# Decoder layer with 160 routed experts: two lists of expert blocks, the first beside the last row; few-pair experts four to a block; weighted y rows scattered by pair

## The chip, the cores and the metric

The kernel runs on one core of a Trainium2 chip. The metric is device time of one execution in microseconds (us); lower is better. The kernel before takes 1595.51 us, the median of three runs (1593.03 to 1595.99).

## What is computed

Eight sequences ("rows", b = 0 to 7) of 256 tokens with 256 features go through a Mamba block, a cross attention with a feed-forward network, and a mixture of experts, each with a residual and a layer norm. All arithmetic is float32. The change touches the third part:

```
logits = x @ router_w.T + expert_bias[None, :]          # 2048 tokens, 160 experts
top_w, top_idx = jax.lax.top_k(sigmoid(logits), 8)
top_w = top_w / (sum(top_w) + 1e-09) * 2.5
...
h1 = silu(einsum('th,eih->eti', x, w_gate))              # 128 hidden units per expert
routed = einsum('eti,ehi->th', h1 * combine.T[:, :, None], w_down)
shared = silu(x @ w_gate_shared.T) @ w_down_shared.T
x = layernorm(x + routed + shared)
```

Each token picks 8 of 160 experts, so there are 16,384 (token, expert) pairs. How they fall on the experts is fixed by the inputs. Counted from the reference's routing:

| pairs of an expert | experts |
|---|---|
| none | 44 |
| at least one | 116 |
| sum over experts of whole blocks of 128 pairs | 97 blocks |
| remainder after whole blocks 1 to 32 | 72 |
| remainder 33 to 127 | 44 |
| whole blocks of 128 from the first six rows alone | 69 blocks |

Whole blocks and remainders together make 97 + 116 = 213 blocks. The trace of the kernel before agrees with this count: its gathers move packets of four token rows, and of the packets that are only partly filled 31 hold one row, 34 two and 23 three, the numbers that these remainders give.

## The kernel before

Three stages follow one another.

The front (up to 905 us) runs a scan over 8 rows times 16 states. While row b is scanned, the later parts of row b-1 (`rest`, a generator that yields some 35 times: output projection, attention, feed-forward, router) are put between the scan's steps by hand: `manual_schedule` fixes the order of PE (TensorE), ACT (ScalarE), DVE (VectorE) and POOL (GpSimd). `rest` ends with the routing of its row: `so_far` holds the number of pairs of each expert so far, `placei` the place of each pair in the table `tab_d` (2048 places per expert), and `scatter` writes the pair numbers there with 16 indirect DMAs a row (L619). After the last scan step the remainder of row 6's `rest` and the whole of row 7's `rest` run alone, then the last 32 scatters.

Then the list of blocks is made (L697 to L779): how many blocks of 128 pairs each expert has, which expert and which table row each block is, and the table rows themselves, fetched by three indirect DMAs `got` (L760).

The block stage runs `USUAL` = 216 blocks in eight lanes. `fetch(i)` reads the expert's number into SP's register, loads its 256 KB of weights `we` by SP (skipped where the lane's previous block had the same expert), and gathers the 128 token rows `xg` with an indirect DMA of POOL (L799). `block(i)` transposes them on PE (`bt`, copied to `bx` by DVE), multiplies by the gate weights (`bh`, `Silu` on ACT into `bg`), multiplies by the down weights (`by`), copies to `bo` by DVE or ACT and stores 128 rows of `y_d` by SP (L827). Blocks 217 and up stand in a `tc.If` that runs only where more than 216 are needed; here 213 are.

Last, for every 128 tokens, eight indirect DMAs on POOL (L903) bring back the eight y rows of each token, and PE sums them, weighted by diagonal matrices `diags` (L909), with the shared expert (L907); then a layer norm and the output.

Of the kernel before, what the change touches and what calls it, by code (L numbers as in the profile page):

```python
# [14 lines left out]
P = 128  # L15
# [19 lines left out]
NBLK = T * TOPK // P + NE  # L35
QB = -(-NBLK // P)
LANES = 8
USUAL = T * TOPK // P + NE // 2 + LANES
PER = T // P
BIG = float(1 << 20)  # L40
# [21 lines left out]
def decoder_layer(  # L62
# [24 lines left out]
    pools = {}  # L87
    small = ctx.enter_context(tc.tile_pool(name="small", bufs=4))
# [8 lines left out]
    y_d = dram.tile([NBLK * P, D], F32, name="y_d")  # L97
    tab_d = dram.tile([NE * T, 1], F32, name="tab_d")

    tab_views = dram_disjoint_views(tab_d, NTT * TOPK)  # L100


    wts_all = keep.tile([P, NTT, TOPK], F32, name="wts_all")
    which_all = keep.tile([P, NTT, TOPK], F32, name="which_all")
    place_all = keep.tile([P, NTT, TOPK], F32, name="place_all")
    first_place = keep.tile([P, NE], F32, name="first_place")
    nc.gpsimd.iota(first_place, pattern=[[T, NE]], base=0, channel_multiplier=0, allow_small_or_imprecise_dtypes=True)
# [7 lines left out]
    pair_no = keep.tile([P, NTT, TOPK], F32, name="pair_no")  # L115
    nc.gpsimd.iota(
        pair_no, pattern=[[P * TOPK, NTT], [1, TOPK]], base=0, channel_multiplier=TOPK,
# [11 lines left out]


    def exps():
        return nc.scalar.preload_act_table_set("natural_log_exp_and_others")

    def scaling(src, name):
# [8 lines left out]
        for c in range(TT):  # L143
            nc.vector.bn_aggr(mv[:, c, :], st[:, c, :])  # L144
        nc.scalar.activation(rs, mv[:, :, 1], AF.Ln, bias=eps)  # L145
# [26 lines left out]
    with ExitStack() as first:  # L172
        wts = first.enter_context(tc.tile_pool(name="wts", bufs=1))
        m1 = first.enter_context(tc.tile_pool(name="m1", bufs=1))
        m2 = first.enter_context(tc.tile_pool(name="m2", bufs=2))
        m3 = first.enter_context(tc.tile_pool(name="m3", bufs=3))
        m4 = first.enter_context(tc.tile_pool(name="m4", bufs=4))
        pools["ps"] = first.enter_context(tc.tile_pool(name="ps_front", bufs=2, space=PSUM))
        acc = first.enter_context(tc.tile_pool(name="acc_front", bufs=2, space=PSUM))
        held = first.enter_context(tc.tile_pool(name="held", bufs=1, space=PSUM))  # L180
        a1 = first.enter_context(tc.tile_pool(name="a1", bufs=1))
        a2 = first.enter_context(tc.tile_pool(name="a2", bufs=2))
        dr = first.enter_context(tc.tile_pool(name="dr", bufs=2, space=bass.MemoryType.DRAM))

# [27 lines left out]
        def fill():  # L212


            w = none.shape[-1]
            v = tab_d.rearrange("(i p n) o -> p i (n o)", p=P, n=w // 2)
            nc.sync.dma_start(v, none[:, None, : w // 2].to_broadcast([P, NE * T * 2 // (P * w), w // 2]))
            nc.sync.dma_start(
                y_d[USUAL * P :, :].rearrange("(p a n) d -> p a (n d)", p=P, n=w // D),
                none[:, None, :].to_broadcast([P, (NBLK - USUAL) * D // w, w]),  # L220
            )
# [3 lines left out]
        exps()  # L225
# [19 lines left out]
        def head(b, xt, made):  # L245
# [35 lines left out]
            for j in range(KI // 2):  # L281
                pz = projected(KI // 2 + j)
                yield
                nc.scalar.copy(sz[:, 2 * j : 2 * j + 2, :], pz)
            nc.scalar.activation(u, u, AF.Silu)
            nc.scalar.activation(sz, sz, AF.Silu)
            exps()
# [33 lines left out]
            nc.scalar.preload_act_table_set("natural_log")  # L321
            nc.scalar.activation(delta, delta, AF.Ln)  # L322
            exps()
# [57 lines left out]
        def rest(b, sz, ya):  # L381
# [77 lines left out]
            nc.scalar.activation(top, top, AF.Identity, scale=-scale)  # L459
            total = small.tile([P, TT], F32, tag="total", name=f"total_{b}")  # L460
# [79 lines left out]
            nc.sync.dma_start(x3_d[b * S : (b + 1) * S, :].rearrange("(c p) d -> p c d", p=P), x3)  # L540
            yield
# [15 lines left out]
            nc.vector.tensor_add(pr, pl, mid(rv[:, R_EB : R_EB + NE], TT))  # L557
            nc.scalar.activation(pr, pr, AF.Sigmoid)
            exps()
# [27 lines left out]
            place = place_all[:, b * TT : (b + 1) * TT, :]  # L587
            placei = small.tile([P, TT, TOPK], mybir.dt.int32, tag="placei", name=f"placei_{b}")
            expert = small.tile([P, TT, TOPK], mybir.dt.int32, tag="expert", name=f"expert_{b}")
            for c in range(TT):  # L590
                at = pn[:, c * NE : (c + 1) * NE]
                key = a1.tile([P, NE], F32, tag="key", name=f"key_{b}_{c}")
                nc.vector.scalar_tensor_tensor(key, at, 1.0, chosen[:, c, :], ALU.add, ALU.mult)
                nc.vector.max(place[:, c, :], key)
# [3 lines left out]
            ordered = which_all[:, b * TT : (b + 1) * TT, :]  # L598
            nc.vector.tensor_copy(ordered, expert)
            scattered.append(scatter(b, placei))  # L600
            yield
            for c in range(TT):
# [7 lines left out]
                nc.vector.tensor_reduce(wts_all[:, i, :], match, AX.X, ALU.add)  # L610
                nc.vector.tensor_scalar(
                    wts_all[:, i, :], wts_all[:, i, :], den[:, c : c + 1], ROUTED_SCALE, ALU.mult, ALU.mult
                )

        def scatter(b, placei):
            for c in range(TT):
                for j in range(TOPK):
# [3 lines left out]
                        in_=pair_no[:, i, j : j + 1], in_offset=None,  # L621
# [14 lines left out]
        E_ = mybir.EngineType  # L636
        with tc.manual_schedule(engines={E_.PE, E_.Activation, E_.DVE, E_.Pool}):
# [4 lines left out]
            ahead = 0  # L642
            for i, (b, n) in enumerate(steps):
# [32 lines left out]
            rests.append(rest(B - 1, made["sz"], made["ya"]))  # L676
            while rests:
                go(rests)
            while scattered:
                go(scattered)  # L680


    I32 = mybir.dt.int32
    blk = ctx.enter_context(tc.tile_pool(name="blk", bufs=1))
    pools["ps"] = ctx.enter_context(tc.tile_pool(name="ps", bufs=4, space=PSUM))
    acc = ctx.enter_context(tc.tile_pool(name="acc", bufs=4, space=PSUM))
    b2 = ctx.enter_context(tc.tile_pool(name="b2", bufs=2))
    b3 = ctx.enter_context(tc.tile_pool(name="b3", bufs=3))
    b4 = ctx.enter_context(tc.tile_pool(name="b4", bufs=4))

    sh = blk.tile([P, KD * P + D], F32, name="sh")
    nc.sync.dma_start(sh, shared)
    nblk = blk.tile([P, NE], F32, name="nblk")
    nblki = blk.tile([P, NE], I32, name="nblki")
    upto = blk.tile([P, NE], F32, name="upto")
    total = bank("total")[:, :NE]
    nc.tensor.matmul(total, ones, so_far, start=True, stop=True)  # L697
    nc.vector.tensor_sub(nblk, total, first_place)
    nc.vector.tensor_scalar_add(nblk, nblk, float(P - 1))
    nc.vector.tensor_copy(nblki, nblk)  # L700
    nc.vector.tensor_single_scalar(nblki, nblki, 7, op=ALU.logical_shift_right)
    nc.vector.tensor_copy(nblk, nblki)
    nc.vector.tensor_tensor_scan(upto, ones[:, 0:1].to_broadcast([P, NE]), nblk, 0.0, ALU.mult, ALU.add)


    moved = blk.tile([P, NE], F32, name="moved")
    nc.vector.tensor_sub(moved, upto, nblk)
    nc.vector.scalar_tensor_tensor(moved, moved, float(P), first_place, ALU.mult, ALU.subtract)
    slot = blk.tile([P, NTT, TOPK], F32, name="slot")
    sloti = blk.tile([P, NTT, TOPK], I32, name="sloti")  # L710


    turn = blk.tile([P, QB], I32, name="turn")
    nc.gpsimd.iota(turn, pattern=[[P, QB]], base=0, channel_multiplier=1)
    lanei = blk.tile([P, QB], I32, name="lanei")
    nc.vector.tensor_single_scalar(lanei, turn, LANES - 1, op=ALU.bitwise_and)
    nc.vector.tensor_single_scalar(turn, turn, LANES.bit_length() - 1, op=ALU.logical_shift_right)
    step = blk.tile([P, QB], F32, name="step")
    nc.vector.tensor_copy(step, turn)
    block_no = blk.tile([P, QB], F32, name="block_no")  # L720
    nc.vector.tensor_copy(block_no, lanei)
    leni = blk.tile([P, 1], I32, name="leni")
    lane_len = blk.tile([P, 1], F32, name="lane_len")
    nc.vector.tensor_scalar_add(lane_len, upto[:, NE - 1 : NE], float(LANES - 1))
    nc.vector.tensor_copy(leni, lane_len)
    nc.vector.tensor_single_scalar(leni, leni, LANES.bit_length() - 1, op=ALU.logical_shift_right)
    nc.vector.tensor_copy(lane_len, leni)
    lane_ends = blk.tile([P, LANES], F32, name="lane_ends")
    for i in range(LANES):
        nc.vector.tensor_scalar_mul(lane_ends[:, i : i + 1], lane_len, float(i + 1))  # L730
    nc.vector.scalar_tensor_tensor(
        block_no, block_no, lane_len, step, ALU.mult, ALU.add
    )
    past = blk.tile([P, QB], F32, name="past")
    nc.vector.tensor_scalar(past, step, lane_len, float(2 * NBLK), ALU.is_ge, ALU.mult)
    nc.vector.tensor_add(block_no, block_no, past)
# [46 lines left out]
    for t in xg:  # L783
        nc.gpsimd.memset(t, 0.0)
# [88 lines left out]
    for i in range(LANES - 1):  # L873
        fetch(i)
    for i in range(USUAL):
# [5 lines left out]
        if i == 8 * NTT:  # L881
            slots()
# [100 lines left out]
```

## Time and profile before

| what | us |
|---|---|
| median of three runs | 1595.51 |
| the profiled execution | 1594.16 |
| its span, first to last instruction | 1592.3 |
| PE busy in the span | 1147.9 (72%) |
| DVE busy | 895.6 (56%) |
| POOL busy | 881.4 (55%) |
| ACT busy | 664.0 (42%) |
| mean granted TensorE clock | 0.852 |

The shares are averages over stages that are bound by different things, so they say little by themselves. Times in the profile count from the start of the span. A group of instructions is listed as line, engine, operation, output<-input, shape and count, then total busy time and mean of one in ns, then the time its engine sat idle just before it and what ended that.

### The profile page before, as it was taken

Reading aid. Unit: us, or ns where it says so; the run is one execution under the profiler, and the core shown is the slowest. Engines: PE = TensorE matmul, PEld = TensorE weight load, DVE = VectorE, ACT = ScalarE, POOL = GpSimd, SP = SyncE. Lnnn points to the kernel's source line nnn. Section 1 sums busy time; section 2 is a strip of 40 time slices with the busy share of each in tenths; the row PEclk is TensorE's granted clock in tenths of the full one; section 3 lists DMA queues with packets and bytes.
Section 4 is the critical chain, followed back from the end, with each engine's and each line's share of the span. In section 5 each row is a group of like instructions: output and inputs, shape, how many; then the busy total and the mean of one; then the engine's idle time right before and its main releaser. Section 6 shows DMA issues by size and latency. Waiting matters only on the chain. (4 is left out here: it accounts for less than half of the span.)

```text
span 1592.3 us, 16270 instructions
## 1 busy us (share of the span) xinstructions
PE 1147.9 (72%) x4283; PEld 751.5 (47%) x4283; DVE 895.6 (56%) x1786; ACT 664.0 (42%) x1532; POOL 881.4 (55%) x713
## 2 busy tenths in 40 slices
PE   4367877787786787787777755038888888877776
PEld 2123544455354454454444444026666666653433
DVE  2478789678668677767868532649633333320000
ACT  4264664744755655654744423002222222212221
POOL 1545464574574655744847302656566666637775
PEclk8588989888798898888888977559999999987776
DMA  9611202112112211111120000036777778644443
GB/s 319 230 60 53 80 34 64 43 60 40 41 60 47 47 47 54 25 55 41 35 71 27 16 5 13 1 100 203 218 223 210 217 209 251 209 130 131 131 133 93
DMA packets 110292, 160.30 MB, mean 101 GB/s; under 512 B 20756, under 2 KB 77622, under 8 KB 110192
## 3 DMA queue, kind: packets, MB, share of 16 engines
q1 hardware_dynamic: 89488, 125.37, 25.5%
q0 software_dynamic: 20704, 33.81, 7.9%
q14 instruction: 63, 0.52, 0.2%
q8 instruction: 37, 0.61, 0.2%
HBM read 152.28 MB, written 43.58 MB: 123 GB/s over the span
## 5 line engine op out<-in xcount | busy, mean ns | idle before, releaser
L373 PE MATMUL ya<-h,ident 128*128 128x512 f32 x512 | 297.2, 711 | 135.2 <-DVE h L368 135.1
L343 POOL TENSOR_TENSOR g<-du,bc 128x1024 f32<-128x1024 f32 x128 | 300.0, 2355 | 95.1 <-DVE states L358 73.9
L358 DVE TENSOR_TENSOR_SCAN states<-decay,g 128x512 f32<-128x512 f32 x256 | 314.5, 1229 | 60.2 <-ACT decay L348 20.9
L348 ACT ACTIVATE decay<-delta,na 128x255 f32<-128x255 f32 x512 | 237.9, 474 | 136.1 <-DVE states L358 125.0
L799 POOL DMA_INDIRECT xg<-x_d,tokens x216 | 216.3, 1001 | 130.6 <-PE bt L810 120.3
L373 PEld LDWEIGHTS ya<-h,ident 128*128 128x128 f32 x512 | 107.6, 223 | 258.4 <-DVE h L368 141.3
L812 DVE COPY bx<-bt 128x256 f32<-128x256 f32 x216 | 92.0, 426 | 179.9 <-PE bt L810 179.1
L821 PE MATMUL by<-we,bg 128*128 128x256 f32 x432 | 151.1, 432 | 44.0 <-ACT bg L819 35.5
L819 ACT ACTIVATE bg<-bh 128x128 f32<-128x128 f32 x216 | 60.0, 278 | 247.3 <-PE bh L815 244.2
L368 DVE TENSOR_TENSOR h<-states,bc 128x1024 f32<-128x1024 f32 x128 | 156.1, 1219 | 4.9
L903 POOL DMA_INDIRECT y<-y_d,sloti x128 | 121.1, 946 | 57.9 <-issue 36.0
L619 POOL DMA_INDIRECT tab_d<-pair_no,placei x128 | 128.9, 1007 | 38.1 <-issue 29.7
L909 PE MATMUL yn<-y,diags 128*128 128x256 f32 x256 | 112.9, 554 | 39.6 <-DMA y<-y_d,sloti 38.4
L815 PEld LDWEIGHTS bh<-bx,we 128*128 128x128 f32 x864 | 129.8, 193 | 20.5 <-DVE bx L812 10.0
L815 PE MATMUL bh<-bx,we 128*128 128x128 f32 x864 | 134.6, 279 | 4.1 <-DVE bx L812 2.8
L821 PEld LDWEIGHTS by<-we,bg 128*128 128x128 f32 x432 | 65.2, 189 | 96.3 <-ACT bg L819 95.7
L909 PEld LDWEIGHTS yn<-y,diags 128*128 128x128 f32 x256 | 56.5, 259 | 93.6 <-DMA y<-y_d,sloti 89.4
L256 PE MATMUL pj<-xt,in_sb 128*128 128x256 f32 x256 | 74.8, 445 | 26.9 <-DVE u L275 14.8
L910 DVE TENSOR_TENSOR xs<-xs,yn 128x512 f32<-128x512 f32 x8 | 5.5, 688 | 157.6 <-PE yn L909 157.6
L810 PE MATMUL bt<-ident,xg 128*128 128x128 f32 x432 | 83.5, 275 | 3.8 <-DMA xg<-x_d,tokens 3.8
L256 PEld LDWEIGHTS pj<-xt,in_sb 128*128 128x128 f32 x256 | 56.5, 226 | 46.3 <-issue 15.8
L324 POOL TENSOR_TENSOR delta<-delta,e 128x1024 f32<-128x1024 f32 x8 | 18.8, 2347 | 97.7 <-ACT delta L322 97.7
(215 smaller groups left out, 1660.0 us busy)
## 6 DMA issues: line engine op xcount, KB each, us to landing
we<-in_experts_dram SPq DMA_DIRECT2D x216, 256.0 KB
bc<-bc_d SPq DMA_DIRECT2D x64, 512.0 KB
y_d<-bo SPq DMA_DIRECT2D x216, 128.0 KB
y_d<-none SPq DMA_DIRECT2D x1, 9216.0 KB
xg<-x_d,tokens POOLq DMA_INDIRECT x216, 3.8
xt<-in_x_t_dram SPq DMA_DIRECT2D x8, 256.0 KB
w_sb<-in_w_dram SPq DMA_DIRECT2D x2, 1024.0 KB
xn<-in_x_dram SPq DMA_DIRECT2D x8, 256.0 KB
```

The lines of the kernel that those rows point to most:

```text
L256: nc.tensor.matmul(pj[:, e, :], in_sb[:, k, o : o + P], xt[:, k, :], start=(k == 0), stop=(k == KD - 1))
L343: nc.gpsimd.tensor_mul(g, made["du"], mid(made["b_rows"][:, n % NG, :], KI))
L348: nc.scalar.activation(decay[k // 2][:, k % 2, 1:], made["delta"][:, k, 1:], AF.Exp, scale=na[:, k * NS + n : k * NS + n + 1],)
L358: nc.vector.tensor_tensor_scan(states_f[:, part], decay[j].rearrange("p k t -> p (k t)"), gf[:, part], 0.0, ALU.mult, ALU.add)
L368: nc.vector.tensor_mul(h, states, mid(made["c_rows"][:, n % NG, :], KI))
L373: nc.tensor.matmul(ya[j], ident, hf[:, j * NT : (j + 1) * NT], start=(n == 0), stop=(n == NS - 1))
L619: nc.gpsimd.indirect_dma_start(out=tab_views[i * TOPK + j], out_offset=bass.IndirectOffsetOnAxis(ap=placei[:, c, j : j + 1], axis=0), in_= ...
L799: nc.gpsimd.indirect_dma_start(out=xg[i % LANES], out_offset=None, in_=x3_d, in_offset=bass.IndirectOffsetOnAxis(ap=tokens[:, i : i + 1], ...
L815: nc.tensor.matmul(ph, w[:, k * P : (k + 1) * P], xt[:, k * P : (k + 1) * P], start=(k == 0), stop=(k == KD - 1))
L821: nc.tensor.matmul(py, g, w[:, KD * P :], start=True, stop=True)
L903: nc.gpsimd.indirect_dma_start(out=y8[:, j, :], out_offset=None, in_=y_d, in_offset=bass.IndirectOffsetOnAxis(ap=sloti[:, i, j : j + 1], a ...
L909: nc.tensor.matmul(pn[:, c, :], diags[:, i, j, :], y8[:, j, :], start=False, stop=(j == TOPK - 1))
```

## The change

Pairs now carry their weight: `pair_all` holds (pair number, weight) and `tab_d` is twice as wide; the weight arithmetic moves ahead of the scatter in `rest`. `y_d` has one row per pair (16,384 rows) in place of one per block slot.

Blocks come from two times and three kinds. List a: whole blocks of 128 pairs of the first six rows, at most `FIRST` = 68, made while row 7 is scanned. List b: the whole blocks that are left after all eight rows, and the remainders above `FEW` = 32 pairs, one block each; 64 of them (`USUAL`) always run. List c: remainders of 1 to 32 pairs, four experts to a block (`GROUP`); 20 such blocks (`USUAL_FEW`) always run. What b and c hold beyond that is run by a `tc.If`, which goes through all the slots that are left of both lists, whatever their number.

After the scan and the remainder of row 6's `rest`, the three first steps of row 7's `rest` run, the scan's memory is given up, and the blocks start. Row 7's `rest`, the scatters of rows 6 and 7 and the making of lists b and c are links of a chain, about one of which is put after each block of list a. One turn `s` issues, in order, the fetch for a later turn, the transposes of turn s+2, the gate product of s+1, the down product of s and the store of s-1. Every block loads its own weights, into 12 buffers; 8 buffers hold gathered rows. The y rows are scaled by the weight when they leave PSUM and are scattered to the row of their pair by an indirect DMA of POOL (the SP store is gone). The shared expert's part is added to `base` beside list b. At the end one plain DMA of 2 MB a row brings the y rows in pair order, and DVE sums the eight of each token.

The core of the diff, with the new functions:

```diff
+AFTER = B - 2
+FIRST = 68
+FEW = 32
+GROUP = P // FEW
+MOST = T * TOPK // P + NE
+USUAL = 64
+USUAL_FEW = 20
...
+    y_d = dram.tile([T * TOPK, D], F32, name="y_d")
+    tab_d = dram.tile([NE * T, 2], F32, name="tab_d")
...
+        def first_list():
...
+            nc.vector.tensor_copy(wholei, counted("a", some))
+            nc.vector.tensor_single_scalar(wholei, wholei, P.bit_length() - 1, op=ALU.logical_shift_right)
...
+            nc.vector.scalar_tensor_tensor(done, done, 0.0, whole, ALU.max, ALU.min)
+            lists["done"] = done
+            yield
+            yield from listed("a", 0, ends, whole, None, P, some, blk)
+        def other_lists(kept, temps):
...
+            nc.vector.scalar_tensor_tensor(cnt, done, float(-P), cnt, ALU.mult, ALU.add)
...
+            nc.vector.scalar_tensor_tensor(nblk, left, float(FEW), whole, ALU.is_gt, ALU.add)
+            upto(ends, nblk)
...
+            nc.vector.tensor_scalar_add(rest_of, ends[:, NE - 1 : NE], float(-USUAL))
+            nc.vector.tensor_scalar_add(few_rest, few_ends[:, NE - 1 : NE], float(-USUAL_FEW * GROUP))
+            nc.vector.tensor_tensor(rest_of, rest_of, few_rest, ALU.max)
+            nc.vector.tensor_scalar(rest_of, rest_of, 0.0, 1.0, ALU.max, ALU.add)
+            resti = kept.tile([P, 1], I32, name="resti")
+            nc.vector.tensor_copy(resti, rest_of)
+            lists["more"] = resti
...
+            def fetch(turn):
...
+                for g in range(needs(turn)):
+                    w = we[used[0] % NW]
...
+                    nc.sync.dma_start(
+                        w, experts[bass.ds(ev, 1), :, :].rearrange("o p n -> p (o n)"),
+                        bounds_check="skip_entire_dma",
+                    )
...
+                nc.gpsimd.indirect_dma_start(
+                    out=xi, out_offset=None, in_=src,
+                    in_offset=bass.IndirectOffsetOnAxis(ap=tokens[:, i : i + 1], axis=0),
...
+            def inner(turn):
...
+                for g, w in enumerate(t["ws"]):
+                    for k in range(KD):
+                        nc.tensor.matmul(
+                            ph[:, g * n : (g + 1) * n], w[:, k * P : (k + 1) * P],
+                            t["xt"][:, k * P + g * n : k * P + (g + 1) * n], start=(k == 0), stop=(k == KD - 1),
+                        )
...
+            def outer(turn, odd):
...
+                for g, w in enumerate(t["ws"]):
+                    nc.tensor.matmul(
+                        py[g * n : (g + 1) * n, :], t["g"][:, g * n : (g + 1) * n], w[:, KD * P :], start=True, stop=True
+                    )
...
+                if odd:
+                    nc.scalar.activation(t["y"], py, AF.Identity, scale=t["wt"])
+                else:
+                    nc.vector.tensor_scalar_mul(t["y"], py, t["wt"])
+            def store(turn):
...
+                nc.gpsimd.indirect_dma_start(
+                    out=y_views[view], out_offset=bass.IndirectOffsetOnAxis(ap=t["pairs"], axis=0),
+                    in_=t["y"], in_offset=None, bounds_check=T * TOPK - 1, oob_is_err=False,
+                )
+            def go_through(turns, between):
+                n = len(turns)
+                fetched = 0
+                for s in range(-2, n + 1):
+                    while fetched < min(n, max(s, 0) + NX - 1) and (
+                        sum(needs(t) for t in turns[max(s, 0) : fetched + 1]) <= NW
+                    ):
+                        fetch(turns[fetched])
+                        fetched += 1
+                    if 0 <= s + 2 < n:
+                        turn_x(turns[s + 2])
+                    if 0 <= s + 1 < n:
+                        inner(turns[s + 1])
+                    if 0 <= s < n:
+                        outer(turns[s], s % 2)
+                    if 0 <= s - 1 < n:
+                        store(turns[s - 1])
+                    between(s)
+            usual = [("a", i) for i in range(FIRST)] + [("b", i) for i in range(USUAL)]
+            usual += [("c", i) for i in range(USUAL_FEW)]
+            chain = [rests, scattered, [other_lists(kept, temps)]]
...
+            go_through(usual, beside)
...
+    more = nc.values_load(lists["more"][0:1, 0:1], min_val=1, max_val=MOST + NE)
+    with tc.If(more > 1):
+        with tc.manual_schedule(engines={E_.PE, E_.Activation, E_.DVE, E_.Pool}):
+            for kind in ("b", "c"):
+                for q in range(1, -(-MOST // P) if kind == "b" else -(-NE // P)):
+                    for _ in listed(kind, q, *lists[kind]):
+                        pass
+            turns = [("b", i) for i in range(USUAL, MOST)] + [("c", i) for i in range(USUAL_FEW, NE // GROUP)]
+            go_through(turns, lambda s: None)
...
+            nc.sync.dma_start(
+                y8, y_d[b * S * TOPK : (b + 1) * S * TOPK, :].rearrange("(c p j) d -> p c j d", p=P, j=TOPK)
             )
+            on = y8s.tile([P, TT, D], F32, tag="on", name=f"on_{b}")
+            nc.vector.tensor_reduce(on, y8.rearrange("p c j d -> p c d j"), AX.X, ALU.add)
+            nc.vector.tensor_add(on, on, lists["base"][:, b * TT : (b + 1) * TT, :])
+            layernorm(on, on, f"on_{b}")
+            nc.sync.dma_start(out[b].rearrange("(c p) d -> p c d", p=P), on)
```

`listed(name, q, ...)` makes up to 128 entries of one list: for each it finds the expert and the table row on DVE, fetches the table rows with one indirect DMA of POOL, transposes them on PE and copies pair numbers, weights and token numbers out of PSUM. `sums(b)` is the shared expert's part of one row. A slot past the end of a list gets numbers outside every bound, so that its DMAs move nothing; its instructions are issued all the same.

## The prediction

> **What bounds the kernel now.** I read the busy time by stage first, because whole-span shares mix stages. Columns: stretch, its length, then busy us (and instructions) of PE, PE weight loads, DVE, ACT, POOL; granted clock, DMA share, GB/s.
>
> ```profile
> 0.00:905.00 905.00, 662.88 (x2058) 409.15 (x2059) 652.27 (x854) 503.02 (x1054) 494.59 (x311) 0.86 0.22 68
> 905.00:929.00 24.00, 8.05 (x24) 5.09 (x22) 8.91 (x40) 8.51 (x20) 3.75 (x5) 0.58 0.10 33
> 929.00:998.00 69.00, 42.74 (x160) 32.83 (x160) 18.20 (x72) 21.57 (x56) 11.36 (x18) 0.80 0.02 8
> 998.00:1060.00 62.00, 3.55 (x11) 2.33 (x11) 29.02 (x181) 1.28 (x1) 35.99 (x38) 0.50 0.03 3
> 1060.00:1420.00 360.00, 306.57 (x1744) 235.19 (x1744) 173.96 (x606) 93.95 (x330) 214.67 (x215) 0.98 0.72 214
> 1420.00:1592.30 172.30, 124.15 (x288) 66.91 (x288) 13.26 (x40) 35.69 (x71) 121.06 (x128) 0.72 0.40 119
> ```
>
> Scan to 905; row 6's remainder to 929; row 7's `rest` alone to 998 (a latency chain, nobody full); 32 scatters and the list to 1060; blocks to 1420, PE 85% busy; return of y to the end, bound by POOL. The groups say what sets the pace of blocks and return:
>
> ```profile
> L799 POOL DMA_INDIRECT xg<-x_d,tokens x216 | 216.3, 1001 | 130.6 <-PE bt L810 120.3
> L903 POOL DMA_INDIRECT y<-y_d,sloti x128 | 121.1, 946 | 57.9 <-issue 36.0
> L619 POOL DMA_INDIRECT tab_d<-pair_no,placei x128 | 128.9, 1007 | 38.1 <-issue 29.7
> L821 PE MATMUL by<-we,bg 128*128 128x256 f32 x432 | 151.1, 432 | 44.0 <-ACT bg L819 35.5
> L815 PE MATMUL bh<-bx,we 128*128 128x128 f32 x864 | 134.6, 279 | 4.1 <-DVE bx L812 2.8
> ```
>
> POOL waits for PE (120.3 us before L799), and PE hardly for anything (4.1 before L815): a block takes what its PE work, L821 and L815 above all, needs. The timeline of POOL shows this pace, and the price of a gather; the last is of block slot 215, past the end of the list of 213, with no row to move:
>
> ```profile
> 1397.81 1.00 POOL L799 DMA_INDIRECT xg<-x_d,tokens  x1 [0.57 <-PE bt L810]
> 1399.38 1.00 POOL L799 DMA_INDIRECT xg<-x_d,tokens  x1 [0.57 <-PE bt L810]
> 1400.95 1.00 POOL L799 DMA_INDIRECT xg<-x_d,tokens  x1 [0.57 <-PE bt L810]
> ```
>
> 1.57 us a block, and an indirect DMA costs POOL 1.00 whether its rows exist or not. Back to back, with nothing to wait for, the pace is 0.30 more (issue), and a read of the table waits for its writes:
>
> ```profile
> 1038.99 0.96 POOL L619 DMA_INDIRECT tab_d<-pair_no,placei  x1 [0.30 <-issue]
> 1041.20 0.95 POOL L619 DMA_INDIRECT tab_d<-pair_no,placei  x1 [1.25 <-DMA tab_d<-pair_no,placei]
> 1049.81 1.04 POOL L760 DMA_INDIRECT got<-tab_d,rowi  x1 [7.66 <-DMA tab_d<-pair_no,placei]
> ```
>
> **How many turns run.** The first thing to settle is the `tc.If`. List a takes 68 of the 69 whole blocks of the first six rows. Of 97 whole blocks 29 remain, and 44 experts have a remainder above 32: list b has 29 + 44 = 73 entries, and 64 always run. List c has 72 experts, 18 blocks of 20. So `more` = max(73 - 64, 72 - 80, 0) + 1 = 10, above 1: the branch is taken. It doesn't run the 9 that are missing: it runs all slots left, 288 - 64 = 224 of kind b and 40 - 20 = 20 of kind c, 235 of these 244 empty. Before, 216 slots covered 213 blocks and the branch was passed over.
>
> **Price of a turn.** Each turn now has two indirect DMAs on POOL, gather and y scatter. Gather: 1.00 + 0.30 = 1.30. A scatter of 1 KB rows is in no row of the trace; the nearest are L619 (4-byte scatter, 0.96 + 0.30 undisturbed, 1.007 + 0.30 mean) and L903 (1 KB gather, 0.95 + 0.30). I take 1.28; bounds 1.25 and 1.45 (gathers beside a busy DVE took up to 1.16). A turn of one expert is then 2.58 us of POOL. PE's 1.57 (at clock 0.98; 2.1 at 0.72), DVE and ACT lie under it. DMA: 256 KB weights, 128 KB in and 128 KB out in 2.58 us are 203 GB/s, under the 214 that the stage reached at share 0.72. So POOL bounds lists a and b, and whatever else POOL does adds.
>
> The Trainium skill speaks against this price: "DMA: Bandwidth & Descriptors", section "Issuing engines are not separate DMA queues", says that the issuing engine's time is usually small beside the DMA itself, so that moving the store from SP to POOL would change little. By that rule a turn would stay at 1.57 and the sum below would come to 2259 - 356 x 1.01 = 1899. L799's row is the measurement, and I go by it.
>
> **The sum on the profiled span (1592.3).**
>
> A, until the first block's gather: row 6's remainder ends at 929.0, the three first steps of row 7's `rest` at 936.7 (end of L409), eight memsets of `xg` 2.7. Making list a adds some 25 DVE instructions of 0.15 to 0.5 us in row 7's scan, where DVE is 72% busy: 3 (0 to 10). Removed table loads and the dropped 9.2 MB fill of `y_d` lie where ACT and DMA have room (0.22 share): nothing; without that room the fill is 29 us at 319 GB/s, a gain. End 943.
>
> B, lists a and b: 132 x 2.58 = 341. Beside them on POOL: row 7's `rest`, six adds and products of 1.27, a cast 0.25, two sums of 0.56: 9; 32 scatters x 1.26: 40; two `got`: 3. The table wait (7.66) stands in POOL's queue, with all later gathers and scatters behind it, and PE's order holds row 7's matmuls between blocks: 12 (0 to 50). The 131 us from 929 to 1060 are otherwise hidden under POOL. Sum 405, end 1348.
>
> C, 20 turns of list c: 1 MB of weights at 214 GB/s is 4.9; only three turns fit the 12 buffers, so a load is sent when the third turn back has left, and SP sends four (0.6 to 0.85 each, by L795's neighbours): I take 6.0. Bounds 2.58 (POOL) and 8. 120, end 1468.
>
> D, the branch: register load and compare 5 (at the old branch PE sat idle 4.5 to 4.9 before L907); three lists one after the other, from first `got` to first gather 8.3 before, 9.3 each with their DVE head: 28; 224 x 2.58 = 578; 20 empty turns of four experts: no weights, PE bounds: 16 gate matmuls 0.11 apart (four L815 take 0.61) to 0.19 (their weight load): 1.8 to 3.0, 8 down matmuls 0.22 apart (L526, 32 in 7.07): 1.8, transposes 0.4; 4.7 taken, 2.58 to 7 as bounds (clock 0.72): 94; filling and draining 8. Sum 713, end 2181.
>
> The skill's page "TensorEngine Tiling (Array Packing)", section "Overview", promises up to four times for operands of at most 32 columns; by it the down products shrink to 0.45 and D by 27 us, the total to 2232. No matmul of the trace has 32 columns, so I leave it out.
>
> E, the end: 172 us go. 16.8 MB of y and 2 MB of output at the 319 GB/s of the first slice: 59. DVE's sum of 4096 values: L610 218 ns for 64, L458 691 for 512, so 1.056 ns a value, 4.5 us; with add and statistics 6.2 a row, 50 in all, under the DMA. First load 4, last row's sum, norm and store 12. 75 (65 to 100, at 214 GB/s).
>
> Span 2256. Outside it lie 1.86 (1594.16 - 1592.3), and the median stands 1.35 above the profiled run: **2259 us**, slower than the median by 663.
>
> **Rivals.** *The branch isn't taken* (my count, or how `more` comes out, is wrong): D falls to 5, 2259 - 708 = 1551, **faster** by 44. For it: everything else in the change hides or removes work (131 + 172 us against B and C). Against: the trace's partly filled packets agree with the count. It decides below 65 entries in b; and as 44 us buy only 17 turns of 2.58, no branch of this form can be afforded.
>
> *Empty turns are cheap*: descriptors past the bounds cost POOL nothing, or PE sets the pace: b turns 1.57, c turns 2.6: 2259 - 226 - 42 = **1991**. Against: slot 215's gather took 1.00.
>
> *The y scatter is dear*: POOL held until y has landed in DRAM, as in the 1.25 and 7.66 waits above. At 1 us more: 356 x 1.0, **2615**. Against: most of L619 follow each other by 0.30.
>
> **Chances.** Forecast 0.80, not taken 0.07, cheap 0.07, dear 0.04, else 0.02. The range adds the open costs: POOL's pace (712 indirect DMAs, -0.03 to +0.1: -21 to +71), list c and its empty turns (-80 to +86), B (-12 to +38), E (-10 to +25), together 2136 to 2479; all of them high at once is unlikely, so 2130 to 2390. The rivals lie outside, with 0.2. Faster by over 0.2% (what a measurement of this kernel tells from no change) 0.07, within it 0.01, slower 0.92.
>
> **What would show it.** After some 1470 us more than 200 turns whose gathers and scatters move almost nothing, POOL alternating L892 and L942 every 1.3, PE waiting for `xg`; got three times in the branch; DMA share near zero there; the tail under 100 us. Wrong, if L892 counts 152 instead of 396 (not taken), if PE instead of POOL is full in lists a and b, or if a turn there lasts over 3 us.

## The result, and the profile after

The changed kernel takes **2264.68 us** (median of 4 runs, 2260.49 to 2266.51) against 1595.34 us of the kernel before in the same measurement (1593.03 to 1595.99): a ratio of 1.4196, 95% interval 1.417 to 1.4221. Slower by 669 us; 663 were forecast, 2259 us. The profiled execution took 2266.51 us with a span of 2264.8.

First the busy time by stage, cut where the stages of this kernel end. Columns as in the prediction: stretch, its length, busy us (and instructions) of PE, PE weight loads, DVE, ACT and POOL; granted clock, DMA share, GB/s.

```profile
0.00:905.00 905.00, 665.38 (x2066) 407.43 (x2066) 648.25 (x879) 503.86 (x1060) 495.73 (x312) 0.87 0.20 60
905.00:940.00 35.00, 15.19 (x44) 11.46 (x44) 8.52 (x35) 8.54 (x16) 8.76 (x16) 0.61 0.14 40
940.00:1350.00 410.00, 266.25 (x1250) 205.60 (x1250) 115.92 (x317) 102.87 (x268) 307.84 (x303) 0.77 0.62 168
1350.00:1470.00 120.00, 100.25 (x524) 81.30 (x524) 15.72 (x44) 12.03 (x32) 44.61 (x44) 0.50 0.57 172
1470.00:2180.00 710.00, 490.19 (x2320) 366.31 (x2320) 169.32 (x407) 126.63 (x367) 502.96 (x490) 0.73 0.03 4
2180.00:2265.00 85.00, 0.00 (x0) 0.00 (x0) 69.06 (x48) 35.71 (x71) 0.00 (x0) 0.50 0.58 222
```

The scan is what it was (905 us). Blocks start at 940 instead of 1060, and the return of y takes 85 us instead of 172. Between them stands a stretch of 710 us that the kernel before did not have, in which the DMAs move 4 GB/s: it works on nothing. The page's bar of 40 slices shows it at one glance (57 us a slice; POOL's busy tenths, then what the DMAs moved):

```profile
POOL 3455565655564753377777773367777777776410
...
GB/s 241 43 75 49 55 43 61 49 64 38 61 47 33 51 53 2 119 164 204 123 142 171 171 162 191 157 37 1 1 1 1 1 1 1 1 1 1 1 154 181
```

POOL's tenths look the same, seven, in list b with its weights and rows and in the branch without them. The groups of the whole span give what POOL does there, and why a busy share of 0.71 can be a full engine:

```profile
L942 POOL DMA_INDIRECT y_d<-bo_b,pairs_b x288 | 296.2, 1029 | 89.7 <-issue 68.0
L892 POOL DMA_INDIRECT xg<-x_d,tokens_b x288 | 295.0, 1024 | 87.8 <-issue 64.6
...
L904 PE MATMUL bt_b<-ident,xg 128*128 128x128 f32 x576 | 152.3, 357 | 253.8 <-DMA xg<-x_d,tokens_b 253.5
```

288 is `MOST`: every slot of list b ran, though the list has 73 entries. Before each indirect DMA stand about 0.30 us that the profile calls issue. The part of the stretch that holds the 224 turns of one expert:

```profile
1485.00:2084.00 599.00, 394.29 (x1814) 289.05 (x1815) 150.78 (x345) 115.35 (x337) 461.47 (x450) 0.78 0.04 5
```

POOL's 450 instructions there make 135 us of issue, and 461 + 135 = 596 of 599. PE waits for the gathered rows. The chain of waits says "DMA" for the same thing:

```profile
DMA 19%; issue 8%; DVE 3%; POOL 3%; PE 1%; POOLq 0%; ACT 0%; ACTq 0%; SPq 0%; DVEq 0%
DMA xg<-x_d,tokens_b 16%; DVE on L1055 2%; DMA y_d<-bo_b,pairs_b 2%; POOL xg L892 2%; POOL y_d L942 1%; PE bt_b L904 1%; DMA y<-y_d 0%; DVE st_on L153 0%; PE bh_b L915 0%; DVE on L1056 0%; PE by_b L929 0%; POOLq L892 0%; POOLq L942 0%; DMA xg<-x_d,tokens_c 0%; DMA y_d<-bo_c,pairs_c 0%
```

A reader who stopped here would speed up a transfer that carries no bytes. POOL's timeline (start, duration, idle before and what ended it) shows the start of the branch and the pace in its middle:

```profile
1463.60 0.98 POOL L942 DMA_INDIRECT y_d<-bo_c,pairs_c  x1 [0.30 <-DMA we<-in_experts_dram]
1466.81 1.05 POOL L702 DMA_INDIRECT got_b<-tab_d,rowi_b  x1 [2.22 <-DVE got_b L701]
1474.20 1.01 POOL L702 DMA_INDIRECT got_b<-tab_d,rowi_b  x1 [6.34 <-DVE got_b L701]
1481.82 0.99 POOL L702 DMA_INDIRECT got_c<-tab_d,rowi_c  x1 [6.62 <-issue]
1483.12 0.99 POOL L892 DMA_INDIRECT xg<-x_d,tokens_b  x1 [0.30 <-issue]
...
1801.53 1.03 POOL L892 DMA_INDIRECT xg<-x_d,tokens_b  x1 [0.30 <-DMA xg<-x_d,tokens_b]
1802.86 1.03 POOL L942 DMA_INDIRECT y_d<-bo_b,pairs_b  x1 [0.31 <-DVE bx_b L906]
1804.19 1.03 POOL L892 DMA_INDIRECT xg<-x_d,tokens_b  x1 [0.30 <-issue]
```

Three `got` for three lists, and then gather and scatter in turn, one every 1.33 us, with no longer idle time between them: 2.66 a turn. PE's timeline of one turn of list c in the branch:

```profile
2122.64 0.69 PE L904 MATMUL bt_c<-ident,xg 128*128 128x128 f32 x2
2123.12 3.46 PE L915 MATMUL bh_c<-bx_c,we 128*128 128x32 f32 x16
2126.51 1.08 PE L929 MATMUL by_c<-we,bg_c 128*32 128x256 f32 x8
2127.52 0.69 PE L904 MATMUL bt_c<-ident,xg 128*128 128x128 f32 x2
```

4.88 us from transpose to transpose, full on PE. The 16 gate products take 0.22 each, at a granted clock of 0.50; the eight down products together take 1.08.

### The profile page after: what moved, and what is told of

Read it like the earlier page. It is cut to its first block, busy times and chain, and to the rows that moved or that the text cites. A ratio compares the mean times of both kernels' runs of the same rounds, so it can differ in the third digit from the quotient of the medians.

```text
span 2264.8 us, 24063 instructions
## 1 busy us (share of the span) xinstructions
PE 1537.3 (68%) x6204; PEld 1072.1 (47%) x6204; DVE 1026.8 (45%) x1728; ACT 789.6 (35%) x1813; POOL 1359.9 (60%) x1163
## 5 line engine op out<-in xcount | busy, mean ns | idle before, releaser
L942 POOL DMA_INDIRECT y_d<-bo_b,pairs_b x288 | 296.2, 1029 | 89.7 <-issue 68.0
L892 POOL DMA_INDIRECT xg<-x_d,tokens_b x288 | 295.0, 1024 | 87.8 <-issue 64.6
L906 DVE COPY bx_b<-bt_b 128x256 f32<-128x256 f32 x288 | 122.2, 424 | 448.9 <-PE bt_b L904 448.6
L904 PE MATMUL bt_b<-ident,xg 128*128 128x128 f32 x576 | 152.3, 357 | 253.8 <-DMA xg<-x_d,tokens_b 253.5
L921 ACT ACTIVATE bg_b<-bh_b 128x128 f32<-128x128 f32 x288 | 79.8, 277 | 584.0 <-PE bh_b L915 583.3
L915 PE MATMUL bh_b<-bx_b,we 128*128 128x128 f32 x1152 | 229.8, 336 | 0.1
L929 PE MATMUL by_b<-we,bg_b 128*128 128x256 f32 x576 | 216.5, 465 | 0.0
L915 PEld LDWEIGHTS bh_b<-bx_b,we 128*128 128x128 f32 x1152 | 209.0, 255 | 0.7 <-DVE bx_b L906 0.3
L635 POOL DMA_INDIRECT tab_d<-pair_all,placei x128 | 129.2, 1010 | 44.4 <-issue 29.2
L915 PEld LDWEIGHTS bh_c<-bx_c,we 128*128 128x128 f32 x640 | 141.4, 333 | 1.6 <-issue 1.6
L915 PE MATMUL bh_c<-bx_c,we 128*128 128x32 f32 x640 | 138.8, 393 | 0.0
L266 PE MATMUL pj<-xt,in_sb 128*128 128x256 f32 x256 | 75.2, 446 | 24.0 <-DVE u L285 11.2
```

The costliest lines, as they stand in the source:

```text
L635: nc.gpsimd.indirect_dma_start(out=tab_views[i * TOPK + j], out_offset=bass.IndirectOffsetOnAxis(ap=placei[:, c, j : j + 1], axis=0), in_= ...
L892: nc.gpsimd.indirect_dma_start(out=xi, out_offset=None, in_=src, in_offset=bass.IndirectOffsetOnAxis(ap=tokens[:, i : i + 1], axis=0), bou ...
L904: nc.tensor.transpose(pt[:, k * P : (k + 1) * P], t["x"][:, k * P : (k + 1) * P], ident)
L906: nc.vector.tensor_copy(t["xt"], pt)
L915: nc.tensor.matmul(ph[:, g * n : (g + 1) * n], w[:, k * P : (k + 1) * P], t["xt"][:, k * P + g * n : k * P + (g + 1) * n], start=(k == 0), ...
L929: nc.tensor.matmul(py[g * n : (g + 1) * n, :], t["g"][:, g * n : (g + 1) * n], w[:, KD * P :], start=True, stop=True)
```

## The experiments

They ran in three sets on three chips; the kernel before took 1591.49, 1629.87 and 1629.85 us there, so times are compared within a set or as ratios to it. The second to the sixth kernel ran once each. Where Silu times are named, a turn's pace is the distance of its Silu (L921) from the next one's.

**Without the branch.** List b of 76 holds the 73 entries, `more` is 1, nothing else differs. Forecast and rival (the change is slow for other reasons too) part here: 1587 us against more than 1700.

```
-USUAL = 64
+USUAL = 76
```

> List b always runs 76 turns instead of 64, so its 73 entries fit and the branch is passed over. Theory (the branch alone makes the kernel slower): its 715 us, from the last store before it to its last store, fall to 5 for the register load and compare, and 12 turns of 2.67 us come on: 2264.8 - 715 + 5 + 32 = 1587 us of span, 0.5% below the kernel before. Rival (the slowness sits in how turns run, branch or not): more than 1700 us.

Measured: 1585.94 us (1575.99 to 1587.36, 7 runs), ratio 0.9951, interval 0.9931 to 0.9972. The branch is the whole of the loss; without it the change gains half a per cent. Four of the kernels below (no scatters, 64 rows, plain store, row 7 first) have this longer list b too.

**16 slots instead of 244 in the branch.**

```
-            turns = [("b", i) for i in range(USUAL, MOST)] + [("c", i) for i in range(USUAL_FEW, NE // GROUP)]
+            turns = [("b", i) for i in range(USUAL, USUAL + 16)]
```

> The branch is taken as in the changed kernel, but goes through 16 slots of list b (64 to 79) and none of list c. Theory (each slot that the branch issues costs its turn, empty or not): 208 turns x 2.64 and 94 us for list c less: 2264.8 - 549 - 94 = 1622 us. Rival (entering the branch, its lists and the refill of the engines are the larger part): above 1700 us.

Measured: 1669.58 us against 1629.87, ratio 1.0244, or 1630 on the scale of the first set, where 1622 was expected. In its trace the branch lasts 66 us, from the last store before it to its own last store; in the changed kernel the same stretch lasts 715. The 649 between them are 208 turns of 2.64 and 20 of 4.9. Ahead of the first gather, for the lists, 18.5 us pass in both. So the loss goes with the slots, and even a branch that barely covers the data loses more than the rest of the change gains.

**The branch without its scatters**, forced though list b has 76 slots; all its turns are empty.

```
-            nc.vector.tensor_scalar(rest_of, rest_of, 0.0, 1.0, ALU.max, ALU.add)
+            nc.vector.tensor_scalar(rest_of, rest_of, 0.0, 2.0, ALU.max, ALU.add)
...
-                    if 0 <= s - 1 < n:
+                    if 0 <= s - 1 < n and keep_y:
...
-            go_through(turns, lambda s: None)
+            go_through(turns, lambda s: None, keep_y=False)
```

> List b runs 76 turns before the branch, the branch is forced, and its 212 + 20 turns, all empty now, don't issue the y scatter. Theory (two indirect DMAs on POOL set the pace): with one, POOL needs 1.33 us a turn and PE sets it at 1.6 to 2.0 us instead of 2.67; the branch shrinks from about 689 us to 460 to 550, the span is 2040 to 2130. Rival (the pace comes from the gather's way to PE, since the chain of waits names the landing of the gather): 2.67 us a turn as before, span about 2270.

Measured: 1961.24 us, below both expectations. The windows of that kernel over part of its branch, and POOL's timeline there:

```profile
1530.00:1800.00 270.00, 254.62 (x1688) 196.68 (x1686) 130.92 (x308) 104.79 (x307) 206.88 (x208) 1.00 0.03 2
```

```profile
1700.18 1.00 POOL L892 DMA_INDIRECT xg<-x_d,tokens_b  x1 [0.30 <-PE by_b L929]
1701.48 1.00 POOL L892 DMA_INDIRECT xg<-x_d,tokens_b  x1 [0.30 <-PE by_b L929]
1702.79 1.00 POOL L892 DMA_INDIRECT xg<-x_d,tokens_b  x1 [0.31 <-PE by_b L929]
```

A turn takes 1.305 us by its Silus: one gather with its issue (POOL: 207 + 208 x 0.30 = 269 of 270). So the scatter is what the other half of a turn was, and the rival that has the gather's way to PE set the pace falls. The expectation was too high because it took PE to need 1.6 to 2.0 us; PE is 94% busy at 1.30, at a granted clock of 1.00. Row L821 of the kernel before shows idle time in its 1.57: PE stood 44.0 us before that line, 35.5 of them for the Silu of the same block, 0.2 us a block. The new order puts other products between a Silu and its down product; what makes the rest, 1.36 against 1.30, no run parts.

The same kernel's turns of four experts, empty too, show something that the changed kernel hides. PE's timeline and two windows at their start:

```profile
1797.58 0.44 PE L904 MATMUL bt_c<-ident,xg 128*128 128x128 f32 x2
1797.86 1.87 PE L915 MATMUL bh_c<-bx_c,we 128*128 128x32 f32 x16
1799.65 0.64 PE L929 MATMUL by_c<-we,bg_c 128*32 128x256 f32 x8
...
1803.48 0.69 PE L904 MATMUL bt_c<-ident,xg 128*128 128x128 f32 x2
1803.96 3.46 PE L915 MATMUL bh_c<-bx_c,we 128*128 128x32 f32 x16
1807.35 1.08 PE L929 MATMUL by_c<-we,bg_c 128*32 128x256 f32 x8
```

```profile
1797.00:1800.00 3.00, 3.00 (x35) 2.35 (x34) 0.82 (x2) 0.46 (x2) 2.39 (x3) 1.00 0.02 0
1803.00:1806.00 3.00, 3.00 (x21) 2.52 (x13) 0.91 (x2) 0.00 (x0) 2.34 (x3) 0.50 0.03 3
```

The first of these turns run at a granted clock of 1.00 and take 2.4 to 2.8 us, about what two indirect DMAs of POOL take (2.66). At about 1802 us, with PE busy without a gap, the clock falls to 0.50, and from then on a turn takes 4.89.

**The price by rows.** The branch's gathers and scatters carry 64 rows instead of 128 (the branch is forced again).

```
-                    out=xi, out_offset=None, in_=src,
-                    in_offset=bass.IndirectOffsetOnAxis(ap=tokens[:, i : i + 1], axis=0),
+                    out=xi[: rows_of[0], :], out_offset=None, in_=src,
+                    in_offset=bass.IndirectOffsetOnAxis(ap=tokens[: rows_of[0], i : i + 1], axis=0),
...
+            rows_of[0] = P // 2
             go_through(turns, lambda s: None)
```

> List b runs 76 turns before the branch, the branch is forced, and its gathers and scatters name 64 rows instead of 128. Theory one (POOL's price goes by the rows that a DMA names): 0.5 + 0.3 each, 1.6 us a turn, span about 2020. Theory two (a price per instruction): 2.64 us a turn, span about 2240.

Measured: 2416.57 us. The total answers nothing: the turns came irregularly, and POOL's stores waited (166 us before L943 in the window below, mostly for DVE and ACT). The price itself can be read from POOL's groups between 1600 and 2200 us of this kernel:

```profile
L893 POOL DMA_INDIRECT xg<-x_d,tokens_b x198 | 186.6, 942 | 61.3 <-issue 42.7 <-PE bt_b L905 10.7 <-remote 3.7
L943 POOL DMA_INDIRECT y_d<-bo_b,pairs_b x198 | 184.9, 934 | 166.3 <-issue 63.1 <-DVE bo_b L937 50.6 <-ACT bg_b L922 50.1
```

942 and 934 ns against the 1024 and 1029 shown above: half the rows save 8 to 9%. POOL's price of an indirect DMA is almost a price per instruction. Why the turns of this run were late (3.02 us in the mean, 2.40 in the median) stays open; PE waited only 1.4 us for gathered rows in this window.

**The store by SP.** y is written in the order of the blocks by a plain DMA that SP issues, so the order by pair, and with it the right sum of each token, is left out.

```
...
-                nc.gpsimd.indirect_dma_start(
-                    out=y_views[view], out_offset=bass.IndirectOffsetOnAxis(ap=t["pairs"], axis=0),
-                    in_=t["y"], in_offset=None, bounds_check=T * TOPK - 1, oob_is_err=False,
-                )
+                nc.sync.dma_start(y_d[view * P : (view + 1) * P, :], t["y"])
```

> List b runs 76 turns and the branch is passed over; y rows are stored by SP in block order, by a plain DMA, so the order by pair is left out of the result. Theory (POOL sets the pace of lists a and b): a turn falls from 2.67 us to between 1.6 (PE) and 2.45 (512 KB at the 214 GB/s of the stage before): over 144 turns 32 to 154 us less than the run with 76 turns, 1433 to 1555. Rival (the issuing engine's time is small beside the DMA itself, so it doesn't matter which engine stores): as the run with 76 turns, about 1587.

Measured: 1431.19 us, 155 below the kernel with list b of 76. A turn of list b falls from 2.70 to 1.61 us in the mean (1.30 in the median, with real rows and weights), one of list a from 3.49 to 2.96. The windows in lists a and b, and in list c:

```profile
1120.00:1220.00 100.00, 84.51 (x512) 70.41 (x512) 54.47 (x133) 45.26 (x111) 60.11 (x61) 0.89 0.87 278
1265.00:1350.00 85.00, 84.50 (x449) 69.25 (x448) 11.57 (x26) 8.50 (x25) 9.18 (x10) 0.50 0.78 235
```

The same bytes go to and fro; POOL drops to 60% (77% in list b of the kernel with 76 turns) and the DMAs rise to 278 GB/s at share 0.87. The prediction weighed a rule of the Trainium skill here ("DMA: Bandwidth & Descriptors", section "Issuing engines are not separate DMA queues": the engine that starts a DMA spends little beside the DMA itself). It doesn't hold for these stores: a scatter holds POOL for 1.03 + 0.30 us even where it moves nothing, and a turn of list b has lost most of that (1.09 us). How much of the 155 us is the engine, and how much that plain rows are written in one piece, this run doesn't part.

**Row 7 before the blocks.** The chain (row 7's `rest`, 32 scatters, the lists) is drained before the first turn instead of beside list a.

```
+            for stages in chain:
+                while stages:
+                    go(stages)
             go_through(usual, beside)
```

> List b runs 76 turns and the branch is passed over; the rest of row 7, the scatters and the making of lists b and c run before the first turn instead of between the turns of list a. Theory (the overlap hides them but for what they ask of POOL): 123 us more ahead of list a, and list a falls from 243 us to 68 x 2.67 = 182: 62 us more than the run with 76 turns, about 1649. Rival (their waits in PE's and POOL's order cost list a as much as they take alone): no difference, about 1587.

Measured: 1628.25 us, 42 above the kernel with list b of 76: two thirds of the 62 that were expected, where the rival had none. In windows:

```profile
940.00:1050.00 110.00, 39.27 (x136) 28.49 (x136) 23.60 (x104) 19.88 (x48) 44.58 (x46) 0.64 0.16 47
1052.00:1222.00 170.00, 109.74 (x533) 81.60 (x532) 44.02 (x100) 34.07 (x100) 130.90 (x129) 0.81 0.66 200
```

The chain alone is 107 us in which nobody is full; list a then takes 172.9 us (Silus) instead of 237.4. The difference, 64.5, is what the chain costs list a when it runs beside it.

**A version that beats both.** Lists sized to the data (73 and 18, no branch), one turn of list c after every fourth of list b, and the sum over the eight rows of y by three halving additions instead of the strided reduction. The first run has all of it; the three of the last set take the edits one at a time and together.

```
+            for i in range(USUAL):
+                usual.append(("b", i))
+                if i % 4 == 3 and i // 4 < USUAL_FEW:
+                    usual.append(("c", i // 4))
...
-            nc.vector.tensor_reduce(on, y8.rearrange("p c j d -> p c d j"), AX.X, ALU.add)
+            nc.vector.tensor_add(y8[:, :, 0:4, :], y8[:, :, 0:4, :], y8[:, :, 4:8, :])
+            nc.vector.tensor_add(y8[:, :, 0:2, :], y8[:, :, 0:2, :], y8[:, :, 2:4, :])
+            nc.vector.tensor_add(on, y8[:, :, 0, :], y8[:, :, 1, :])
```

> List b runs exactly 73 turns and list c 18, the branch is passed over; after every fourth turn of list b stands one of list c; the eight y rows of a token are summed by three adds of halves instead of one reduction with strided reads. From the run with 76 turns (1585.6): 3 turns of b and 2 of c less, -18. Theory (POOL bounds b while PE and the weights bound c, so that mixing covers one by the other): 91 turns x 2.67 = 243 us, or 267 by the DMA rate of 214 GB/s, instead of 291: -24 to -48. Adds: 4.4 us instead of 7.04 a row, or 6.6 by DMA: -4 to -21. Together 1498 to 1540. Rival (at the half clock that list c was granted, mixed turns slow all of PE): no gain by mixing, about 1550 to 1565.

Measured: 1575.55 against 1629.87, ratio 0.9689, interval 0.9648 to 0.9729: faster than both kernels, but less than expected.

> Lists sized to the data (73 and 18 always run, no branch) and one turn of list c after every fourth turn of list b; the sum over the eight rows of y as in the change. Theory (POOL's two indirect DMAs a turn bound list b, PE's weight loads bound list c, so that the two hide each other when mixed): against list b of 76 and c of 20 one after the other (1585.94 on the first chip) this takes away 3 x 2.70 + 2 x 5.59 = 19 us of turns, and b and c together become (73 + 18) x 2.65 = 241 us instead of 73 x 2.70 + 18 x 5.59 = 298: -57. 1510 us on the scale of 1591.5 for the kernel before, ratio 0.95; up to 0.975 if the landing of the gathers is as late as in the mixed run before. Rival (each turn keeps its own price wherever it stands): only the 19 us, ratio 0.985.

Measured: ratio 0.9677, interval 0.9647 to 0.9708 (1579.11 against 1629.85).

> Lists sized to the data (73 and 18, no branch), not mixed; the sum over the eight rows by three halving adds of contiguous rows instead of one strided reduction. Theory (the return is bound by DVE's reduction, 7.04 us a row against 4.2 for the adds): the tail falls from 87 to 74-76 us, where the DMA bounds it, so 1586 - 19 - 12 = 1555, ratio 0.977. Rival (the transfers of y set the tail): only the 19 us, ratio 0.985.

Measured: ratio 0.9795, interval 0.9762 to 0.9827 (1596.65).

> Both edits at once (the same program as the mixed run before): the two savings add, 1510 - 12 = 1498 on the scale of 1591.5, ratio 0.94 to 0.97 (it was 0.969 when measured first); at least 0.005 below each of the two alone. Rival (the savings overlap): no better than the mixed lists alone.

Measured: ratio 0.9612, interval 0.958 to 0.9644 (1566.3). The three kernels over lists b and c, in windows; first the mixed lists, then the lists one after the other with the additions (b, c, and the return), then both edits (lists, and the return):

```profile
1215.00:1490.00 275.00, 207.89 (x1051) 164.37 (x1050) 59.86 (x139) 45.66 (x135) 174.41 (x171) 0.73 0.60 181
```

```profile
1215.00:1430.00 215.00, 147.89 (x633) 111.54 (x631) 50.31 (x115) 37.19 (x112) 145.78 (x142) 0.73 0.51 153
1430.00:1520.00 90.00, 81.28 (x428) 66.26 (x427) 11.15 (x25) 8.22 (x24) 32.84 (x32) 0.50 0.64 194
1522.00:1594.00 72.00, 1.38 (x16) 0.28 (x8) 46.99 (x65) 37.47 (x73) 1.98 (x2) 0.50 0.69 265
```

```profile
1215.00:1490.00 275.00, 210.66 (x1094) 163.99 (x1093) 62.05 (x142) 47.38 (x141) 181.19 (x177) 0.75 0.61 186
1490.00:1561.00 71.00, 0.41 (x2) 0.00 (x1) 46.84 (x65) 37.42 (x73) 2.51 (x3) 0.53 0.70 271
```

Mixing is worth 29 us by the Silus (b and c from 310.5 to 281.5), half of the 57 expected; the two kernels with the additions, which differ in the mixing alone, lie 30 us apart, so the rival (nothing from mixing) falls. In the mixed lists POOL with its issue times is at 174 + 171 x 0.30 = 226 of 275, PE at 208, so neither is full. What fills the rest isn't shown; on this chip list b alone isn't full on POOL either (146 + 142 x 0.30 = 188 of 215), though the expectation priced it as if it were. With the additions the return, from the last store to the end, takes 68 us, where the mixed lists without them take 88; the DMAs run at 265 to 271 GB/s, and most of the third in which DVE is free lies ahead of the first row and behind the last. Both edits together lie 12.8 us below mixing alone, where 12 were expected; as the return alone became 20 shorter, that match is partly chance.

## Why the prediction was right

The forecast case came, and the span missed by 9 us (2264.8 against 2256). The stages missed by -6.5, +16, -14, +2 and +11, so a good part of the closeness is luck. The terms, by the steps of the sum:

- **The branch is taken**, with 244 slots: shown by L892's count for list b, by the run without the branch and by the one with 16 slots. The rival of 1551 us comes close to what the kernel without the branch takes (1585.94): that one runs 12 turns more in list b (12 x 2.7 = 32).
- **Price of a turn.** 2.58 forecast; 2.64 in the mean in the branch. The gather (1.02 + 0.30) and the scatter (1.03 + 0.30) cost the same; the scatter's 1.28 from the 4-byte scatters was 0.05 low. The rival of dear scatters falls by the timeline, that of cheap empty turns by L892's 1024 ns.
- **PE's pace** was misread. The prediction let PE need 1.57 us a block, as PE hardly waited (4.1 us before L815); but its own row of L821 has PE idle 44.0 us before the down products. PE needs at most 1.30 at a full clock. Nothing followed from it in the sum, since POOL set the pace, but the expectation for the branch without scatters was too high by it, and with it the 1991 us of the rival with cheap turns.
- **A**, 936.5 instead of 943: row 6's remainder ended at 926.6 instead of 929.0, the 3 us for row 7's longer scan weren't needed, and the memsets ran beside PE's third step.
- **B**, 421 instead of 405, end 1357.6 instead of 1348. The other work beside list a was sized at 52 + 12 = 64, and the kernel with row 7 first shows 64.5 in all (its parts weren't measured). What is missing is turns of 2.72 instead of 2.58 in list b (64 x 0.14 = 9), and some 8 between the first gather and the first Silu, which the sum had for the branch and not for list a.
- **C**, 106 instead of 120. The weights were thought to bound it, with SP's four issues a turn; PE does, at clock 0.50. In the kernel with the plain store these turns take 4.9 us with their weights, as long as the empty ones, with PE busy 84.5 of 85 us. In the changed kernel they take 5.5 by their Silus, and what is over 4.9 is PE waiting for gathered rows (nine times, 11.2 us in all).
- **D**, 715 instead of 713, of two errors that cancel: the lists 20 instead of 33 (one `got` every 7.4 to 7.6 us, and no 5 us for the compare), the 224 turns 592 instead of 578. The 20 turns of four experts were right at 94, but by their parts not: gates 3.5 instead of 1.8 to 3.0, down products 1.08 instead of 1.8. The gates are long by the clock: at 1.00 the branch without scatters shows them in 1.87, within what the prediction had, but the lowest clock that it reckoned with was 0.72, and 0.50 was granted. That these errors cancel is luck. The rule that the prediction left out for want of a row (the Trainium skill, "TensorEngine Tiling (Array Packing)", section "Overview": operands of at most 32 columns can share the array, up to four at a time) is borne out by the eight products in 1.08 us at half the clock: four of them start within 0.02 us, the next four 0.43 us later. At clock 1.00 they take 0.64 (the branch without scatters), where the prediction's reckoning by the rule was 0.45. The turn isn't shorter by it, as its gates took longer than thought.
- **E**, 86 instead of 75, and here the step failed in its cause. The prediction put DVE's sum at 4.5 us a row by 1.056 ns a value, under the DMA. The groups from 2180 us on in the changed kernel, and from 1490 on in the version with both edits:

```profile
L1055 DVE TENSOR_REDUCE on<-y 128x512 f32<-128x4096 f32 x8 | 56.3, 7039 | 11.7 <-DMA y<-y_d 11.7
```

```profile
L1058 DVE TENSOR_TENSOR y<-y 128x2048 f32<-128x2048 f32 x8 | 18.2, 2271 | 15.4 <-DMA y<-y_d 15.4
L1059 DVE TENSOR_TENSOR y<-y 128x1024 f32<-128x1024 f32 x8 | 9.8, 1226 | 0.3
L1060 DVE TENSOR_TENSOR on<-y 128x512 f32<-128x512 f32 x8 | 5.5, 692 | 0.6
```

The strided reduction takes 7.04 us, 1.72 ns a value; DVE is busy 69 of 85 us and waits for a transfer once, so DVE bounds the return and the DMAs, at 222 GB/s, follow. The additions take 4.19 us. DVE still goes from row to row almost without a wait, one every 5.9 us (of its 15.4 us of waiting 13.4 are the first load), but now the DMAs beside it are as good as full. Two windows of the version with both edits:

```profile
1514.00:1524.00 10.00, 0.00 (x0) 0.00 (x0) 9.79 (x15) 7.52 (x14) 0.00 (x0) 0.50 0.94 349
1524.00:1534.00 10.00, 0.00 (x0) 0.00 (x0) 9.61 (x17) 7.42 (x15) 0.00 (x0) 0.50 1.00 395
```

So the two are level there. That DVE lies under the DMA, as the prediction had it, no run shows; the transfers go faster than the 319 GB/s that it took.

One part of the range doesn't follow from the bounds given: list c and its empty turns at 2.58 us each would be some 110 us less (20 x 3.42 + 20 x 2.12), not 80. Nothing hangs on it, as the result lies near the middle.

## What to carry to other kernels

A branch that covers the worst case costs its issued instructions, not its data: count its slots, price a slot by the engine that must issue it, and compare with what the change saves elsewhere before asking how often it is taken; here the list was 9 entries short and 244 slots ran. An indirect DMA of 128 rows was work of its issuing engine here, some 1.33 us whether its rows moved or not, so two of them per block replaced a PE bound by a POOL bound; the chain of waits that blamed a DMA at 4 GB/s meant its issuer. Two loops with different bounds (POOL here, PE there) were worth mixing, but brought half of the overlap that the prices of their turns promised.

## What the runs showed of the hardware

- The granted clock is 0.50 in the turns of four experts, with weights (1350 to 1470) and empty, though PE is busy without a gap where it falls from 1.00 (about 1802 us in the branch without scatters). In that kernel's empty turns of one expert it is 1.00 at 94% busy. So a busy PE alone didn't keep the clock here; whether the small products or the weight loads between them are the reason wasn't tried.
- An empty indirect DMA costs POOL as much as a full one (1.03 both), and half the rows only 8 to 9% less.
- The strided reduction over the middle axis took 1.72 ns a value, where the addition of 2048 values in whole rows took 1.11 (2271 ns).
- On the chips of the second and third set list a took 267 to 284 us instead of 237, with the same indirect DMAs (1.03). What makes it longer wasn't found; PE's waits for gathered rows are not longer there (12 us in the kernel with 16 slots, 41 in the one with list b of 76).
